# A planned attention and feed-forward block on one core: first loads keep their ranks, transfers reckoned at 0.26 MB per us, head norms off VectorE, the planner's rank shifts sought anew

## The chip, the core and the metric

The kernel runs on one core of a Trainium2 chip. The metric is the device time of one execution in microseconds (us), lower is better. Five engines work beside each other, each through its own list of instructions in a fixed order: TensorE (PE in the profile, with PEld for its weight loads), VectorE (DVE), ScalarE (ACT), GpSimd (POOL) and SyncE (SP), which here only issues DMA transfers. The engines meet through semaphores alone, so an instruction starts when its engine reaches it and every semaphore that it names has the wanted count.

## The reference

One transformer block with post-layernorm, in fp32, for 2 sequences of 512 tokens and a model width of 512.

```python
q = (x @ Wq.T)  # 32 heads of 128;  k, v: 8 heads of 128 (4 query heads share one)
q = q * rsqrt(mean(q*q) + 1e-6) * q_norm_w        # per token and head, k likewise
scores = q @ k.T / sqrt(128) + slope[head] * (key - query), keys after the query masked
out = softmax(scores) @ v @ Wo.T
x = layernorm(x + out)
h = silu(x @ gate_w.T * gate_s) * (x @ up_w.T * up_s)      # width 1376, weights are int32
x = layernorm(x + h @ down_w.T * down_s)
```

## The kernel before, in words

**Work and its pieces.** The attention part is cut by KV head `g` (0 to 7), sequence `b` (0, 1) and block `i` of 128 queries (0 to 3); a `unit` is one (g, b, i), and two neighbouring blocks make a `pair` `p`. For a pair, the projections to q, k and v are matmuls of 128 x 384; they are made by a seven-product scheme (`seven`, L747, PSUM banks `pa_q`, `pb_q`, `pc_q`), whose sums of inputs (`sx`, `tq`, and for the output projection `so`, `si`, `to`, `ti`) VectorE or GpSimd make as `tensor_tensor` operations, all at L688. The very first pair is projected plainly (`project_plain`, L867, banks `pp`). Sums such as `xT<-xT` are made in place, so a product that reads that tile waits for them.

**A head's norm.** `heads` squares a pair's projections on ScalarE (L1002), sums them per head on VectorE (L1025, tile `ms`), takes the power -0.5 on GpSimd (L674, tile `inv`), and multiplies each row by its norm: one `tensor_tensor` of 128 x 640 on VectorE or GpSimd (L1072), or five activations of 128 x 128 with a scale on ScalarE (L1065). There are 32 pairs with 2 row blocks each, so 64 such steps. The result is turned in 32 x 32 squares on VectorE (L1188) and brought into place through DRAM (`far_q` L1201, `qT` L1212).

**Scores to output.** For each unit: four score matmuls (`sc`, L1263), bias and row maximum on VectorE (L1272), exponential on ScalarE (L1288), division on ScalarE or GpSimd (L1320, L1322), squares turned on VectorE (L968, tile `st`), a trip through DRAM (`far` L977, then two loads `prT` L1385), and the product with v on TensorE (`pa`, L1408). The first units are transposed on TensorE instead (`pt`, L1359). Then the output projection (`pa_o` and its like), layernorm, and the feed-forward part (`pa_h`, `pa_d`).

**Who decides the order.** Nothing of the order is written by hand. Every operation is added to a list (`Work.add`) with a rank (`prio`; lower is earlier), the engines that may run it with a cost on each, and what it depends on. `Work.order` then plays the list through, engine by engine, with these costs: at each step it takes the operation that can start first, among equals the one of lowest rank, and so fixes both the engine and the place of each operation. DMA transfers share one lane in this play: each is reckoned at its size in MB divided by a rate, after 2.0 us of start. `Work.emit` writes the instructions in that order. Before the play, `Work.shift` is called once for each number in `SHIFTS`: the number seeds a generator that picks a stretch of ranks and adds small random amounts to the ranks in it. The numbers thus decide the order of all engines in the attention part and beyond. The lines that a sentence can't say:

```python
at, reach, by = rnd.uniform(-9, 100), rnd.choice((1, 3, 8, 30)), rnd.choice((0.1, 0.3, 1.0))
NORMED = {"DVE": dve(5 * HD) + 0.2, "POOL": pool_tt(5 * HD), "ACT": 5 * act(HD, True)}
WHO = ("DVE", "POOL", "ACT")
W.add({k: mb / 0.3 for k in queues}, prio, lambda e: fn(engine[e]), reads, writes, after)
```

**The start.** The first weights `w` (six parts on SP's queue, L486: two halves of the first quarter of depth, then the quarters), the first tokens `xT` (L512, on ScalarE's queue and later SP's), the norm weights `qw`, `kw` (L559, L560), the output weights `wo` (L541) and the tokens `acc` (L1674) have the ranks from -9.0 to -8.3. While they come, TensorE runs 14 transposes of the identity (`warm`, L554).

Of the kernel before, what the change touches and what calls it, by code (L numbers as in the profile page):

```python
# [60 lines left out]
def act(n, scaled=False):  # L61
    return 0.15 + 0.00084 * n + (0.1 if scaled else 0.0)


def dve(n):
    return 0.15 + 0.00106 * n


def pool_tt(n):
    return 0.27 + 0.00197 * n  # L70


def pool_ts(n):
# [3 lines left out]
LAG = {"PE": 0.22, "DVE": 0.1, "ACT": 0.12, "POOL": 0.2, "SP": 0.1, "ACTQ": 0.1, "NONE": 0.0}  # L77
TABLE = 1.28
SHIFTS = (
    42000001, 42000003, 42000019, 42000038, 42000046, 42000048, 42000080, 42000095, 42000168,  # L80
    42000176, 42000217, 42000257, 42000262, 42000308, 42000360, 42000448, 42000460, 42000471,
    42000478, 42000488, 42000493, 42000503, 42000508, 42000510, 42000517, 42000520, 42000530,
    42000532, 42000548, 42000582, 42000707, 42000844, 42000865, 42000884, 42000922, 42000957,
    42000970, 42000975, 42001005, 42001037, 42001049, 42001090, 42001148, 42001238, 42001283,
    42001404, 42001444, 42001471, 42001476, 42001778, 42002042, 42002048, 42002090, 42002122,
    42002149, 42002330, 42002340, 42002665, 42002784, 42002821, 42003002, 42003036, 42003133,
    42003139, 42003188, 42003348, 42003694, 42003791, 42004290, 42004466, 42005040, 42005857,
    42006497, 42006735, 42006892, 42007003, 42007117, 42007158, 42007651, 42008481, 42008514,
    42009150, 42011723, 42012356, 42012546, 42013135, 42013648, 42014108, 42014321, 42014614,
    42014976, 42015318, 42015996, 42016788, 42016932, 42017026, 42017104, 42017164, 42020579,  # L90
    42020641, 42021783, 42021971, 42022454, 42022740, 42023193, 42023363, 42024350, 42024865,
    42025415, 42026349,
)
NORMED = {"DVE": dve(5 * HD) + 0.2, "POOL": pool_tt(5 * HD), "ACT": 5 * act(HD, True)}
WHO = ("DVE", "POOL", "ACT")
ALONE = lambda p, r: False


# [65 lines left out]
class Work:  # L164
# [166 lines left out]
    def shift(self, seed):  # L331

        rnd = random.Random(seed)
        at, reach, by = rnd.uniform(-9, 100), rnd.choice((1, 3, 8, 30)), rnd.choice((0.1, 0.3, 1.0))
        moved = {}
        for o in self.ops:
            if abs(o["first"] - at) < reach:
                key = o["first"], tuple(sorted(o["costs"]))
                if key not in moved:
                    moved[key] = rnd.gauss(0, by)  # L340
                o["prio"] += moved[key]

    def emit(self):
        for seed in SHIFTS:
# [9 lines left out]
def post_ln_block(  # L354
# [22 lines left out]
    W = Work()  # L377
# [93 lines left out]
    def load(mb, prio, fn, writes, reads=(), queue="SP", after=()):  # L471
        engine = {"SP": nc.sync, "ACTQ": nc.scalar}
        queues = (queue,) if isinstance(queue, str) else queue
        W.add({k: mb / 0.3 for k in queues}, prio, lambda e: fn(engine[e]), reads, writes, after)

    w_qkv, w_o, t_q, t_o, t_i = {}, {}, {}, {}, {}

    def load_qkv(g, prio):
        w = Buf(r_w, f"w_{g}")
        w_qkv[g] = w  # L480

        def columns(kc, ns, at, queue="SP"):
            load(
                0.2 * len(ns),
                at,
                lambda q: q.dma_start(  # L486
                    w[:, kc, ns[0] : ns[-1] + 1, :], wqkv[g, :, kc, ns[0] : ns[-1] + 1, :]
                ),
                [(w, (n, kc)) for n in ns],
                queue=queue,  # L490
            )

        for kc in range(NK):
            at = prio + 0.01 * kc
            if g == 0:
                load_x(0, 0, (kc,), at, "ACTQ", 1 if kc else 2)
            if g == 0 and kc == 0:

                columns(kc, (0,), at)
                columns(kc, (1,), at + 0.001)  # L500
            else:
                columns(kc, (0, 1), at)

    def load_x(b, q, kcs, prio, queue="SP", parts=1):

        k0, k1 = kcs[0], kcs[-1] + 1
        n = NTH // parts
        for k in range(parts):
            load(
                0.13 * len(kcs) / parts,  # L510
                prio + 0.0001 * k,
                lambda e, c=k * n: e.dma_start(  # L512
                    xT[b][:, k0:k1, q * NTH + c : q * NTH + c + n], xt[b, q, :, k0:k1, c : c + n]
                ),
                [
                    (xT[b], (kc, 2 * q + m))
                    for kc in kcs
                    for m in range(k * n // P, (k + 1) * n // P)
                ],
                queue=queue,  # L520
            )
# [8 lines left out]
    def load_o(g, prio):  # L530
        if g == HKV - 1:

            flat = lambda t: t.rearrange("p j n c -> p (j n c)")[:, : 4 * DM]
            view = lambda t: flat(t).rearrange("p (m k c) -> p m k c", m=4, k=2)
            wo = Buf(r_ti, f"wo_{g}", view)
            after = [o for t in t_i.values() for o in t.users]
        else:
            after = []
            wo = Buf(r_wo, f"wo_{g}")
        w_o[g] = wo  # L540
        load(1.05, prio, lambda q: q.dma_start(wo[:, :], wot[g]), [(wo, m) for m in range(4)], after=after)  # L541
# [60 lines left out]
    order, first, past = Buf(r_prT, "order"), Buf(r_prT, "first"), Buf(r_prT, "past")  # L602
# [383 lines left out]
    def heads(p, prio):  # L986
# [67 lines left out]
        for r in range(2):  # L1054


            def normed(e, r=r):
# [16 lines left out]
            W.add(  # L1074
                {k: NORMED[k] for k in WHO},
                prio,
# [980 lines left out]
    for fc in range(NF):  # L2057
# [10 lines left out]
            after=[finished[EARLY + fc - 1]],  # L2068
# [12 lines left out]
            after=pace,  # L2081
        )
    for c in range(KF):
# [7 lines left out]
            after=[finished[EARLY + NF + c]],  # L2091
# [152 lines left out]
```

## Time and profile before

| what | value |
|---|---|
| median of 3 runs | 952.7 us (951.93, 952.7, 955.5) |
| the profiled execution, its own time | 954.71 us |
| its span, from the first to the last instruction | 952.9 us |
| mean granted TensorE clock | 0.997 |
| TensorE busy (matmul) | 940.2 us, 99% of the span, 4254 instructions |
| VectorE, ScalarE, GpSimd busy | 713.3, 485.2, 549.3 us |
| bytes moved by DMA | 157.46 MB, mean 165 GB/s |

The span is 1.8 us shorter than the time of the same execution. A row of the profile names a line, an engine and an operation, then `out<-in` by tile, shapes and a count; a number in ns is the mean of one instruction, and "idle before, <-releaser" is time in which the engine stood still just before, with what ended it. fp32 matmuls appear as two instructions each, transposes on TensorE as one. The columns of the page's slices give TensorE's granted clock in tenths, so an idle stretch and a slow clock can be told apart.

### The profile page before, as it was taken

Reading aid. Unit: us, or ns where it says so; the run is one execution under the profiler, and the core shown is the slowest. Engines: PE = TensorE matmul, PEld = TensorE weight load, DVE = VectorE, ACT = ScalarE, POOL = GpSimd, SP = SyncE. Lnnn points to the kernel's source line nnn. Section 1 sums busy time; section 2 is a strip of 40 time slices with the busy share of each in tenths; the row PEclk is TensorE's granted clock in tenths of the full one; section 3 lists DMA queues with packets and bytes.
Section 4 is the critical chain, followed back from the end, with each engine's and each line's share of the span. In section 5 each row is a group of like instructions: output and inputs, shape, how many; then the busy total and the mean of one; then the engine's idle time right before and its main releaser. Section 6 shows DMA issues by size and latency. Waiting matters only on the chain.

```text
span 952.9 us, 14098 instructions
## 1 busy us (share of the span) xinstructions
PE 940.2 (99%) x4254; PEld 682.6 (72%) x4254; DVE 713.3 (75%) x1767; ACT 485.2 (51%) x1347; POOL 549.3 (58%) x608
## 2 busy tenths in 40 slices
PE   8999999999999999999999999999999999999997
PEld 5655776766767675767677766676677888888886
DVE  7777877778877878887878888787776766675464
ACT  3676665656565656465746566565652433433100
POOL 5774775657494837775768686866564412232040
PEclk9999999999999999999999999999999999999999
DMA  9269758555583847657678786569852323310011
GB/s 324 67 199 258 232 157 241 170 184 174 176 234 107 267 132 222 206 186 198 172 239 225 235 214 190 174 184 263 217 176 81 86 81 89 85 52 23 1 45 44
DMA packets 196876, 157.46 MB, mean 165 GB/s; under 512 B 28384, under 2 KB 179680, under 8 KB 195520
## 3 DMA queue, kind: packets, MB, share of 16 engines
q1 hardware_dynamic: 195936, 155.90, 54.8%
q8 instruction: 34, 0.56, 0.2%
q10 hardware_dynamic: 864, 0.66, 0.2%
q14 instruction: 42, 0.34, 0.1%
HBM read 97.60 MB, written 58.46 MB: 164 GB/s over the span
## 4 chain that ended last, share of the span: by engine, by line
PE 96%; DMA 2%; SPq 1%; DVE 0%; issue 0%; POOLq 0%; DVEq 0%
PE pa_q L747 17%; PE sc L1263 13%; PE pa L1408 12%; PE pb_q L747 8%; PE pa_h L747 8%; PE pa_o L1632 8%; PE pb_h L747 4%; PE pc_q L747 4%; PE pb_o L1632 4%; PE pa_d L747 4%; PE pa_o L747 3%; PE pc_o L1632 2%; PE pc_h L747 2%; PE pb_d L747 2%; PE px L1440 2%; DMA prT<-far 2%
## 5 line engine op out<-in xcount | busy, mean ns | idle before, releaser
L1288 ACT ACTIVATE pr<-pr,nmax 128x48 f32<-128x48 f32 (+15 forms) x256 | 133.4, 522 | 91.2 <-DVE nmax L1272 90.1
L1263 PE MATMUL sc<-kT,qT 128*128 128x512 f32 (+15 forms) x512 | 154.1, 409 | 0.0
L1272 DVE CUSTOM_DVE_ANT_0 pr<-sc,bias 128x48 f32<-128x48 f32 (+15 forms) x256 | 109.7, 442 | 34.3 <-PE sc L1263 31.5
L1408 PE MATMUL pa<-prT,v 128*128 128x512 f32 (+1 forms) x306 | 129.6, 512 | 2.7 <-DMA prT<-far 2.7
L1263 PEld LDWEIGHTS sc<-kT,qT 128*128 128x128 f32 x512 | 88.2, 191 | 48.2 <-issue 21.9
L1320 ACT ACTIVATE pr<-pr,rden 128x64 f32<-128x64 f32 (+12 forms) x221 | 95.4, 495 | 23.1 <-DVE rden L1303 22.8
L688 DVE TENSOR_TENSOR acc<-acc,pa_o 128x512 f32<-128x512 f32 (+2 forms) x128 | 72.7, 568 | 44.9 <-PE pa_o L1632 28.2
L968 DVE STREAM_TRANSPOSE st<-pr 128x512 f32<-128x512 f32 (+1 forms) x153 | 92.1, 634 | 1.6 <-ACT pr L1320 0.6
L747 PE MATMUL pa_q<-tq,sx 128*128 128x384 f32 x248 | 90.3, 487 | 0.0
L1408 PEld LDWEIGHTS pa<-prT,v 128*128 128x128 f32 x306 | 54.0, 191 | 24.3 <-issue 6.4
L674 POOL TENSOR_TENSOR inv<-ms,nhalf 128x10 f32<-128x10 f32 (+1 forms) x33 | 64.9, 1966 | 7.8 <-DVE ms L1039 5.4
L848 ACT COPY gu<-pa_h 128x256 f32<-128x256 f32 (+1 forms) x88 | 31.8, 370 | 73.3 <-PE pa_h L747 62.7
L1002 ACT ACTIVATE sq<-c 128x640 f32<-128x640 f32 x64 | 45.7, 730 | 38.3 <-DVE c L1188 32.9
L747 PEld LDWEIGHTS pa_q<-tq,sx 128*128 128x128 f32 x248 | 45.5, 190 | 26.9 <-issue 5.5
L848 ACT COPY c<-pa_q 128x384 f32<-128x384 f32 x73 | 34.5, 473 | 54.2 <-PE pa_q L747 47.4
L1065 ACT ACTIVATE sq<-c,inv 128x128 f32<-128x128 f32 x165 | 51.9, 397 | 15.0 <-POOL inv L674 15.0
L1188 DVE STREAM_TRANSPOSE c<-sq 128x320 f32<-128x320 f32 x124 | 55.8, 485 | 0.0
L1025 DVE TENSOR_REDUCE ms<-sq 128x5 f32<-128x640 f32 x64 | 51.4, 810 | 1.2 <-ACT sq L1002 1.2
L1632 PEld LDWEIGHTS pa_o<-ti,si 128*128 128x128 f32 x336 | 43.1, 192 | 7.2 <-issue 3.6
L688 POOL TENSOR_TENSOR so<-aT,aT 128x512 f32<-128x512 f32 x23 | 29.3, 1274 | 32.8 <-PE pa_o L1632 31.7
L1322 POOL TENSOR_SCALAR pr<-pr,rden 128x64 f32<-128x64 f32 (+7 forms) x67 | 31.1, 473 | 29.4 <-DVE rden L1303 28.3
L1288 ACT ACTIVATION_READ_ACCUMULATOR pr<-pr,nmax 128x1 f32 x256 | 48.0, 188 | 0.0
(245 smaller groups left out, 2216.9 us busy)
## 6 DMA issues: line engine op xcount, KB each, us to landing
far<-st SPq DMA_DIRECT2D x122, 256.0 KB, 3.1
prT<-far SPq DMA_DIRECT2D x244, 128.0 KB, 3.2
far_q<-c SPq DMA_DIRECT2D x31, 640.0 KB, 3.9
qT<-far_q SPq DMA_DIRECT2D x62, 320.0 KB, 3.8
w<-in_wqkv_dram SPq DMA_DIRECT2D x39, 384.0 KB, 4.6
wo<-in_wot_dram SPq DMA_DIRECT2D x10, 1024.0 KB, 5.8
far<-st SPq DMA_DIRECT2D x31, 128.0 KB, 2.7
prT<-far SPq DMA_DIRECT2D x62, 64.0 KB, 3.0
```

What stands on the lines that cost most here:

```text
L674: lambda e: nc.gpsimd.tensor_tensor(dst(), src(), nhalf[:, :n], ALU.pow),
L688: lambda e: vec[e].tensor_tensor(dst(), a(), b(), alu),
L747: nc.tensor.matmul(bank[:rows, :width], lhsT=a(fa, c), rhs=b(fb, c), start=(fresh and c == 0), stop=(c == depth - 1), skip_group_check=True,)
L848: nc.scalar.copy(dst(), src())
L968: {"DVE": dve(n)}, prio, lambda e: nc.vector.transpose(dst(), src()), reads, [A(st)]
L1188: lambda e, r=r, m=m: nc.vector.transpose(cb[:, m] .rearrange("p n w -> p (n w)")[:, :half] .rearrange("p (m r h d) -> p r h m d", m=2, r= ...
L1263: lambda e, a=a, w=w, sc=sc: nc.tensor.matmul(sc[:, :w], lhsT=qT[:, r, a, : G * Q], rhs=kT[:, :w], start=True, stop=True),
L1272: lambda e, a=a, w=w, sc=sc: nc.vector.tensor_tensor_reduce(out=pr[:, a, :w], in0=sc[:, :w], in1=bias[:, S - w :], scale=-(SHRINK**-g), sc ...
L1288: lambda e, a=a, w=w: nc.scalar.activation(pr[:, a, :w], pr[:, a, :w], AF.Exp, bias=nmax[:, a : a + 1], scale=-1.0, accum_out=den[:, a : a ...
L1320: nc.scalar.activation(dst, src, AF.Copy, scale=rden[:, a : a + 1])
L1408: lambda e, j=j, prT=prT, n=n: nc.tensor.matmul(by_head(po.tile)[:, :, P - n // G :], lhsT=v[:, j, :], rhs=late(prT, j, n), start=(j == 0) ...
L1632: nc.tensor.matmul(bank[:, ts(c, P)], lhsT=a(fa, c), rhs=b(fb, c), start=fresh and c == 0, stop=True, skip_group_check=True,)
```

## The change

Four edits, of which three only feed the planner:

- the 110 numbers in `SHIFTS` are replaced by 92 others
- `Work.shift` leaves operations alone whose first rank is -8 or lower: the first loads, `warm` and their like keep the ranks that the code gives them
- `load` reckons a transfer at 0.26 MB per us instead of 0.3
- `WHO` no longer offers VectorE for a head's norm (L1072)

No operation is added or taken away. Lines from 341 on stand one line lower in the changed file; lines are named here by the file before.

```diff
 SHIFTS = (
-    42000001, 42000003, 42000019, 42000038, 42000046, 42000048, 42000080, 42000095, 42000168,
...
+    103000003, 103000004, 103000005, 103000010, 103000019, 103000029, 103000038, 103000046,
...
 )
 NORMED = {"DVE": dve(5 * HD) + 0.2, "POOL": pool_tt(5 * HD), "ACT": 5 * act(HD, True)}
-WHO = ("DVE", "POOL", "ACT")
+WHO = ("POOL", "ACT")
...
                 if key not in moved:
                     moved[key] = rnd.gauss(0, by)
-                o["prio"] += moved[key]
+
+                if o["first"] > -8:
+                    o["prio"] += moved[key]
...
-        W.add({k: mb / 0.3 for k in queues}, prio, lambda e: fn(engine[e]), reads, writes, after)
+        W.add({k: mb / 0.26 for k in queues}, prio, lambda e: fn(engine[e]), reads, writes, after)
```

## The prediction, made before the changed kernel was run

> **What bounds the kernel now.** I read the page's engine shares first, then who made TensorE wait, then the timeline where it waited.
>
> ```profile
> PE 940.2 (99%) x4254; PEld 682.6 (72%) x4254; DVE 713.3 (75%) x1767; ACT 485.2 (51%) x1347; POOL 549.3 (58%) x608
> ...
> PE pa L1408 <- DMA prT<-far: 2.7, 2, 2.1
> PE pp L867 <- DMA w<-in_wqkv_dram: 1.8, 1, 1.8
> PE warm L554 <- POOL ident masks.py:199: 1.3, 1, 1.3
> PE pb_q L747 <- DVE ms L1039: 0.5, 1, 0.5
> ```
>
> The last columns of the waits are total, times, longest. TensorE waits 6.7 us of 952.9; everything else is its own work, and no matmul is added or removed. So a new order can win little: the waits at the start (2.2 us with a 0.44 shown further below, not counting `warm`), the two on `prT`, and what the second of these costs behind it:
>
> ```profile
> 685.65 0.33 PE L1263 MATMUL sc<-kT,qT 128*128 128x64 f32 x2
> 688.09 2.05 PE L1408 MATMUL pa<-prT,v 128*128 128x512 f32 x2 [2.11 <-DMA prT<-far]
> ...
> 688.00:689.00 1.00, 0.92 (x1) 0.50 (x2) 0.00 (x0) 0.00 (x0) 0.00 (x0) 0.50 1.11 348
> ...
> 691.00:692.00 1.00, 1.00 (x4) 0.80 (x4) 0.05 (x1) 0.37 (x2) 0.00 (x0) 0.79 0.06 21
> ```
>
> In the stretches the third column from the right is the granted clock. After 2.11 us of waiting it is 0.50 for some 3.4 us, which loses 1.7 us more: 3.8 us in one place. Its cause, from the transfers of 670 to 692 us against the page:
>
> ```profile
> wo<-in_wot_dram SPq DMA_DIRECT2D x1, 1024.0 KB, 8.1
> prT<-far SPq DMA_DIRECT2D x7, 128.0 KB, 6.9
> ...
> prT<-far SPq DMA_DIRECT2D x244, 128.0 KB, 3.2
> ```
>
> A 1 MB `wo` issued at 677.6 us, right ahead of the `prT` loads, made these land in 6.9 us, not 3.2.
>
> **The start, -2.2 us.** In the built order the six `w` parts stand on SP by depth with `qw` and `kw` behind them, and ScalarE's queue has the two 128-wide `xT` parts first. Before, a 256-wide one was first and `qw`, `kw` stood ahead of a `w` part:
>
> ```profile
> 4.52 0.43 SPq L559 DMA_DIRECT2D qw<-in_qnw_dram  x1
> 5.00 0.43 SPq L560 DMA_DIRECT2D kw<-in_knw_dram  x1
> 5.47 0.43 SPq L486 DMA_DIRECT2D w<-in_wqkv_dram  x1
> ...
> 5.04 3.06 PE L867 MATMUL pp<-w,xT 128*128 128x384 f32 x8 [0.44 <-DMA xT<-in_xt_dram]
> 9.87 0.88 PE L867 MATMUL pp<-w,xT 128*128 128x384 f32 x2 [1.77 <-DMA w<-in_wqkv_dram]
> ```
>
> Changed, the first products can start when `warm` ends (1.34 + 3.25 = 4.6 us; the first transfers land at 0.72 + 3.41 = 4.1), and the last `w` part, issued near 4.6 instead of 5.47, lands near 9 us, before the 12th product asks for it at about 12 us. Both waits go: 0.44 + 1.77. Bounds -1.5 and -2.4. The loads moved back are due later: `qw`, `kw` feed only the scaling of k; the next group's `w` now stands behind the four `acc` loads, whose whole chain had landed by 27.5 us before, and is used near 43 us.
>
> **The first seven-product, +0.15 us.** `pb_q` needs `xT<-xT` from VectorE. There TensorE waited 0.51 until 20.93. It now comes 2.2 us earlier, at 18.2. VectorE's list ahead of that sum has four memsets of `pr`, four of `acc`, the bias, the `w`, `tq` sums, two `ms`: with the rows before (0.81 a sum of squares, 1.25 a `tq`, 1.82 on GpSimd between them) its end comes near 18.7, so the wait is about 0.65. GpSimd has one 1.2 us bias step ahead of the first `tq`. Bounds 0 and +1.5.
>
> **The fourth projection, +1.9 us.** New order on TensorE: `pb_q` of pair 2, six transposes, two `pa`, `pb_q` of pair 3. Between, four square turns on VectorE (1.6 us back to back from the 485 ns row, half of them after TensorE's `pb_q`), `c<-pb_q` 0.55, a `ti` sum 0.69, then GpSimd's `ti` 1.27 and `xT<-xT` 0.73, which `pb_q` needs: about 4.2 us after the first `pb_q`, against 0.7 us of transposes and 1.3 us of `pa`. So two waits, 0.5 on ScalarE's copy of `prT` and 1.7 on GpSimd. The 0.25 us that TensorE stood before a score matmul near 55 us goes. Behind the wait stand only matmuls; VectorE and ScalarE have other work. Bounds +0.5 and +2.5.
>
> **One bank used twice running, +0.8 us.** The built order has `pa_q` of pair 27 as four matmuls in a row (two products into one bank); before, none stands so. Between them: the matmul's end (0.17 behind the last issue), ScalarE's copy 0.48, two semaphores (0.04 and 0.14, as seen after such waits). Bounds 0.6 and 1.5.
>
> **`wo` moved, -3.4 us.** The second `wo` of g = 6 now stands six transfers ahead of the turns of that unit, some 14 us before the `prT` loads which it held up. The 0.61 at 648 and the 3.8 at 688 go; the same unit's `prT` stay the tightest of the new order, and I leave 1.0 there (bounds 0 and 2.4).
>
> **Norms.** 7 of 64 leave VectorE, GpSimd has 31 instead of 24, ScalarE keeps 33. The rows:
>
> ```profile
> L1072 POOL TENSOR_TENSOR sq<-c,inv x24: 1250/1256/1346, 49.4 to 666.1; 128x640 f32<-128x640 f32 x24
> L1072 DVE TENSOR_TENSOR sq<-c,inv x7: 817/820/2434, 38.9 to 523.5; 128x640 f32<-128x640 f32 x7
> ```
>
> So 0.44 us more for each of seven, 3.1 in all, on an engine busy 58%, while 26 sums go the other way to VectorE (0.42 to 0.57 us each, 75% busy). One of VectorE's seven took 2.43. The Trainium skill ("GPSIMD Engine Reference", § 4.1 Engine selection) speaks against this move: elementwise work with two inputs belongs on VectorE, GpSimd being about twice slower. The row says 1.53 times. By the rule the seven would cost 0.82 more each, 5.7 us. Either is hidden behind TensorE's next products as long as a pair is projected well ahead; without that cover 3.1 is the bound, and -1.6 the other (that one slow case). I take 0.
>
> **Rank shifts, 0.26.** They have no cost of their own beyond the order. Of waits that an order shows only on the chip I allow +1.0: the size of the 0.61 and 0.44 above.
>
> **The clock.** The Trainium skill ("TensorE: Matmul & The Clock Gate", Part 1) lets the clock drop after an idle window of about 3.4 us. The row shows it after 2.11; after 1.77 at 8.1 us none. By the rule the new 1.7 us wait costs only itself, by the row it is just below. I take 0, with +1.7 in the range.
>
> Sum: -2.2 + 0.15 + 1.9 + 0.8 - 3.4 + 0 + 1.0 = -1.75 against the profiled execution. That one took 954.7, two above the median; the runs lie in twos, near 952.3 and 955.1, and the gap is about what the `prT` wait and its slow clock cost. If the median lacks that cost, the change is worth +1 against it; if the profile adds a constant, -1.75. I take the middle, -0.7: **952.0 us**, its own range 949 to 955.
>
> **The rivals.**
> - *Two `wo` in a row* (slower). The first `wo` of g = 7 and of g = 6 now stand side by side on SP, 2 MB ahead of `far` and `prT` of unit (7, 0, 2). They wait for the last use of g = 5's weights; from there to the product that reads the new `wo` the order has seven 1.29 us products and some score matmuls, 11.1 us. One load took 5.8 (median) to 8.1, the second adds 1.05 / 0.27 = 3.9: 9.7 to 12.0. It decides once 2 MB need more than 11 us. Then some 2.5 us of waiting, 1.7 of slow clock and another 2.1 where the delayed `prT` are read: +6.3, 958.3. For it: 8.1 was seen beside turns. Against: few turns fall there.
> - *VectorE and GpSimd behind at the start*. If `pb_q` waits 2.0 and the fourth projection's wait also halves the clock: +1.35 + 1.7 + 1.7, 956.8.
> - *No surprise, and the 3.8 us is in the median too* (faster): 952.7 - 2.2 - 3.4 + 0.7 with the new waits at their lower bounds, near 947.3.
> - That the change does not do what it says is out: the built order has the loads by rank and no norm on VectorE.
>
> **How the numbers follow.** The forecast has 0.63, the two `wo` 0.17, the start 0.13, the faster case 0.07. This kernel's measurement tells 0.5% (4.8 us) from no change. The first rival falls above 957.5, of the start a quarter: slower 0.20; faster 0.07; the rest 0.73. The range takes in the start rival and most of the two `wo`: 948.5 to 958.5.
>
> **What would show it.** Right: no TensorE wait between 5 and 17 us, one of 0.3 to 1 before the first `pb_q`, about 1.7 on GpSimd's `xT` near 43 us, 0.8 on ScalarE's copy near 545, no clock of 0.50 after the start. Wrong: a wait on `wo` or `prT` near 635 to 650, a half clock behind any wait, or many small waits of scores on `kT` (norms late).

## The result, and the profile after

The changed kernel is slower by a little: median 955.21 us of 17 runs (954.07 to 957.76) against 952.70 of 17 (951.62 to 955.50), ratio 1.0029, 95% interval 1.0021 to 1.0038, which is +2.8 us (+2.0 to +3.6). The forecast was 952.0, a gain of 0.7 against the median. In the profiled executions alone there is a gain, of 0.64: 954.07 against 954.71. That difference between two profiles and two medians is half of this story.

The engines' shares on the page of the changed kernel, and its list of TensorE's waits (total, times, longest):

```profile
PE 939.7 (99%) x4254; PEld 681.8 (72%) x4254; DVE 715.4 (75%) x1772; ACT 480.9 (50%) x1334; POOL 536.0 (56%) x616
```

```profile
PE pb_q L748 <- DVE xT L689: 1.8, 1, 1.8
PE pb_q L748 <- POOL xT L689: 1.5, 1, 1.5
PE warm L555 <- POOL nhalf L548: 1.3, 1, 1.3
PE pa L1409 <- DMA prT<-far: 1.2, 1, 1.2
PE pa_q L748 <- ACT c L849: 0.6, 1, 0.6
PE pa L1409 <- ACT prT L849: 0.2, 1, 0.2
```

The waits on `w` and on the first `xT` are gone, as is one of the two on `prT`. In their places stand two on sums `xT`, one on a copy of `pa_q` and a short one on a copy of `prT`. TensorE waits 6.6 us where it waited 6.7. The timeline shows where the longer ones are:

```profile
20.46 1.53 PE L748 MATMUL pb_q<-w,xT 128*128 128x384 f32 x4 [1.79 <-DVE xT L689]
...
47.04 1.56 PE L748 MATMUL pb_q<-w,xT 128*128 128x384 f32 x4 [1.51 <-POOL xT L689]
...
552.64 1.56 PE L748 MATMUL pa_q<-tq,sx 128*128 128x384 f32 x4 [0.57 <-ACT c L849]
...
690.51 2.33 PE L1409 MATMUL pa<-prT,v 128*128 128x512 f32 x4 [1.20 <-DMA prT<-far]
```

The first line matters most. Before, the first `pb_q` began at 20.93 us, behind 2.2 us of waiting for loads and 0.51 for its sum; now it begins at 20.46. Of the 2.2 us only 0.47 have survived by then. VectorE's list in front of it says why:

```profile
11.72 2.04 DVE L689 TENSOR_TENSOR sx<-xT 128x256 f32<-128x256 f32 x1
...
18.70 0.82 DVE L1026 TENSOR_REDUCE ms<-sq 128x5 f32<-128x640 f32 x1 [0.90 <-ACT sq L1003]
19.43 0.55 DVE L689 TENSOR_TENSOR c<-pc_q,c 128x384 f32<-128x384 f32 x1
19.90 0.41 DVE L689 TENSOR_TENSOR xT<-xT 128x256 f32<-128x256 f32 x1
```

The sum `xT<-xT` needs nothing but the tokens and the first `sx`, both there by 13.8 us. It stands behind a norm's sum `ms`, which waits 0.90 for ScalarE's squares, and these wait for TensorE's last two plain products:

```profile
16.57 0.81 PE L868 MATMUL pp<-w,xT 128*128 128x384 f32 x2
```

They end at 17.38 us, before the change at 17.85: 0.47 sooner, as `pb_q` is. So the chain to the sum moved by 0.47 and not by 2.2, for two reasons. The first products ran slowly (the last section has the numbers: 1.2 us lost, against 0.3 before), and the new order puts a product into `pa_q`, 1.3 us long, ahead of these two.

### The profile page after: what moved, and what is told of

Its sections match the earlier page's. It is cut to its first block, busy times and chain, and to the rows that moved or that the text cites. A ratio compares the mean times of both kernels' runs of the same rounds, so it can differ in the third digit from the quotient of the medians.

```text
span 952.3 us, 14118 instructions
## 1 busy us (share of the span) xinstructions
PE 939.7 (99%) x4254; PEld 681.8 (72%) x4254; DVE 715.4 (75%) x1772; ACT 480.9 (50%) x1334; POOL 536.0 (56%) x616
## 4 chain that ended last, share of the span: by engine, by line
PE 97%; DVE 1%; SPq 1%; POOL 0%; DMA 0%; ACT 0%; issue 0%; POOLq 0%; DVEq 0%
PE pa_q L748 17%; PE sc L1264 13%; PE pa L1409 11%; PE pb_q L748 8%; PE pa_o L1633 8%; PE pa_h L748 8%; PE pc_q L748 4%; PE pb_h L748 4%; PE pb_o L1633 4%; PE pa_d L748 4%; PE pa_o L748 3%; PE pc_h L748 2%; PE pc_o L1633 2%; PE pb_d L748 2%; PE px L1441 2%; PE pb_o L748 1%
## 5 line engine op out<-in xcount | busy, mean ns | idle before, releaser
L1289 ACT ACTIVATE pr<-pr,nmax 128x368 f32<-128x368 f32 (+15 forms) x256 | 133.6, 523 | 77.1 <-DVE nmax L1273 75.3
L1264 PE MATMUL sc<-kT,qT 128*128 128x48 f32 (+15 forms) x512 | 152.0, 407 | 0.0
L1273 DVE CUSTOM_DVE_ANT_0 pr<-sc,bias 128x368 f32<-128x368 f32 (+15 forms) x256 | 110.5, 442 | 33.8 <-PE sc L1264 30.2
L1321 ACT ACTIVATE pr<-pr,rden 128x64 f32<-128x64 f32 (+12 forms) x208 | 90.9, 499 | 18.1 <-DVE rden L1304 17.7
L849 ACT COPY c<-pa_q 128x384 f32<-128x384 f32 x90 | 42.5, 474 | 84.1 <-PE pa_q L748 73.1
L1323 POOL TENSOR_SCALAR pr<-pr,rden 128x64 f32<-128x64 f32 (+9 forms) x80 | 36.8, 472 | 42.4 <-DVE rden L1304 35.4
L748 PE MATMUL pb_q<-w,xT 128*128 128x384 f32 x124 | 45.3, 488 | 3.3 <-DVE xT L689 1.8
L849 ACT COPY aT<-pa 128x512 f32<-128x512 f32 (+1 forms) x46 | 24.3, 529 | 46.5 <-PE pa L1409 40.0
```

What stands on the lines that cost most here:

```text
L748: nc.tensor.matmul(bank[:rows, :width], lhsT=a(fa, c), rhs=b(fb, c), start=(fresh and c == 0), stop=(c == depth - 1), skip_group_check=True,)
L849: nc.scalar.copy(dst(), src())
L1264: lambda e, a=a, w=w, sc=sc: nc.tensor.matmul(sc[:, :w], lhsT=qT[:, r, a, : G * Q], rhs=kT[:, :w], start=True, stop=True),
L1273: lambda e, a=a, w=w, sc=sc: nc.vector.tensor_tensor_reduce(out=pr[:, a, :w], in0=sc[:, :w], in1=bias[:, S - w :], scale=-(SHRINK**-g), sc ...
L1289: lambda e, a=a, w=w: nc.scalar.activation(pr[:, a, :w], pr[:, a, :w], AF.Exp, bias=nmax[:, a : a + 1], scale=-1.0, accum_out=den[:, a : a ...
L1321: nc.scalar.activation(dst, src, AF.Copy, scale=rden[:, a : a + 1])
```

## The experiments

Each kernel below takes the order that `Work.order` returns (the list `placed`) and moves a few operations in it, just before `Work.emit` writes it out; nothing is planned anew unless it is said. `move(a, behind=b)` stands for

```python
placed.remove(at[a])
placed.insert(placed.index(at[b]) + 1, at[a])     # at[n]: the n-th operation that was added
```

and the operations are named in the comment. Ratios are to the kernel before, run on the same chip; where an experiment changes the changed kernel, its gain is the difference of the two ratios, times 952.7. The changed kernel's own 1.0029 comes from other runs than these, so such a gain is good to some 1.2 us either way.

**One load elsewhere (`b_wo_behind`).** The kernel before, for the step "`wo` moved".

```diff
+move(3643, behind=3797)    # second wo of g = 6; the last prT load of unit (6, 1, 2)
```

> The kernel before, with one load moved: the second wo of g = 6 is issued behind the six prT loads of unit (6, 1, 2) instead of ahead of them. Theory P (the prediction's step): the 2.1 us wait on prT near 688 us and the half clock behind it were in the median too, so both go and the median falls by 2.5 to 3.8 us, to 949 to 950. Theory Q: the profiled execution was an unlucky one and the median hardly held this cost: the trace shows the wait gone, the median stays within 0.7 us of 952.7.

Measured: 951.82 against 952.39, ratio 0.9993 (0.9987 to 1.0), -0.7 us. The unit's own `prT` no longer keep TensorE waiting. The next unit's do; its `far` writes are issued just behind the load:

```profile
682.68 0.60 SPq L549 DMA_DIRECT2D wo<-in_wot_dram  x1
684.85 3.04 SPq L985 DMA_DIRECT2D far<-st  x3
...
694.03 1.10 PE L1416 MATMUL pa<-prT,v 128*128 128x512 f32 x2 [0.87 <-DMA prT<-far]
```

So a cost of 3.8 us that goes with the load was not in the median (theory Q, at the edge of what it allowed), and part of what was there only moved: 1.4 us of waits on `prT` are left in this trace, 0.56 near 648 and 0.87 at 694. Three other traces have the order of before at this place. In `b_first_loads` and `b_norms` the wait is 1.5 us and the clock stays at 1.00. In `b_start` it is 1.86 with a clock of 0.50 behind it, in an execution of 955.02 against a median of 952.99. The bad case is thus real, but not the usual one.

**The same load, later still (`b_wo_later`).**

```diff
+move(3643, behind=3830)    # behind the fourth prT load of unit (6, 1, 3)
```

> The kernel before, with the second wo of g = 6 issued later still: behind the first four prT loads of unit (6, 1, 3). In b_wo_behind the load only held up the turns of that next unit instead (a new wait of 0.9 at 693 us). If the load is what makes either unit late, both waits go and the time is 1.5 to 2.3 below before, near 950.5: this is then what the place costs in the median. If the turns are late without it: no more than 0.6 below before, as in b_wo_behind.

Measured: 952.27 against 952.67, ratio 0.9997 (0.9989 to 1.0005): no difference. The trace has one wait on `prT` of 1.2 us, now until 698. The expectation of 1.5 or more fell. In three positions the load leaves 2.1, 0.9 and 1.2 us of waiting on some `prT` near it, and moving it alone earns at most 1.2 us.

**The first loads alone (`b_first_loads`).** The kernel before with only this part of the change: `w` by depth ahead of `qw` and `kw`, `xT` by depth.

```diff
+# SP: six w by depth, qw, kw, then as before; ScalarE's queue: five xT by depth
```

> The kernel before, with only the first loads in the changed kernel's order: w by depth ahead of qw and kw, xT by depth with the 128-wide parts first. The prediction's step: the two waits of TensorE at 5.0 and 9.9 us go and the time falls by 2.2. Rival: the first pb_q is held by the chain of VectorE and GpSimd (in the changed kernel it began at 20.46 us, before at 20.93), so TensorE only waits later: its waits ahead of pb_q grow from 0.5 to 1.5 or 2.2 and the time falls by 0 to 0.7.

Measured: 952.46 against 952.39, ratio 1.0 (0.999 to 1.001). No gain. The waits for loads shrank to 0.2, and the wait at `pb_q` grew from 0.5 to 1.7, as the list of waits shows. The second line is from VectorE's timeline:

```profile
PE pb_q L761 <- DVE ms L1053: 1.7, 1, 1.7
...
10.98 1.50 DVE L582 SCALAR_TENSOR_TENSOR kw<-kw,qw 128x1 f32<-128x1 f32 x1 [1.08 <-DMA kw<-in_knw_dram]
```

Here there is even a second cost: `kw` lands later, and VectorE, which has its scaling ahead of the bias and of the sums, stands still for 1.08 us.

**The chain freed, in the kernel before (`b_start`).**

```diff
+# the first loads as in b_first_loads, and
+move(155, behind=70)    # sx, on GpSimd ahead of the bias steps
+move(156, behind=71)    # xT, on VectorE ahead of the tq sums
+move(157, ahead of 47)  # sx, on GpSimd
+move(49, behind=81)     # one bias step behind the first inv
```

> The kernel before with the first loads in the changed kernel's order (as b_first_loads, which gained nothing) and four sums moved up: sx, xT, sx of the first pair's partner ahead of the bias steps on GpSimd and of the tq sums on VectorE, one bias step behind the first inv. If the chain to xT was all that kept the earlier loads from paying, the wait of 1.7 at the first pb_q goes and the time falls by 1.3 to 1.8, to about 950.9. If something else is due at 18 us (the norm, the transposes of q), TensorE waits there and it stays within 0.6 of before.

Measured: 952.99 against 952.67, ratio 1.0005 (0.9996 to 1.0014). The first `pb_q` no longer waits, but the next two products do, 1.1 and 0.7, for VectorE's copy of `pa_q` and ScalarE's norm. The second answer held: in this order the sum is not the only thing on VectorE that is late.

**The chain freed, in the changed kernel (`a_xt_early`).** Its VectorE has the scaling of `kw` behind the bias and never waits for that load.

```diff
+move(156, behind=155)   # xT, right behind the first sx, on VectorE
+move(157, behind=156)   # the next sx
+move(94, behind=163)    # the first transposes of q, behind the next product
```

> The changed kernel, with the in-place sum xT and the sx behind it moved up on VectorE's list, right behind the first sx at 11.7 us (they need nothing later), and the first transposes of q put behind the next product on TensorE. If VectorE's order alone made the first pb_q wait, its 1.8 us go and the time falls by 1.5 to 1.9 against the changed kernel, to about 953.5. If the lost time comes back at a later wait of the same chain (the norm, the first scores), by under 0.5.

Measured: 954.6, ratio 1.0016 (1.0008 to 1.0023), so -1.2 against the changed kernel, less than the 1.5 to 1.9 expected but within the error of such a difference. In the trace the wait is gone whole and none stands behind it at the start:

```profile
13.82 0.42 DVE L701 TENSOR_TENSOR xT<-xT 128x256 f32<-128x256 f32 x1
...
18.81 1.45 PE L760 MATMUL pb_q<-w,xT 128*128 128x384 f32 x4
20.10 1.45 PE L760 MATMUL pa_q<-tq,sx 128*128 128x384 f32 x4
```

**The fourth projection (`a_xt3`).**

```diff
+move(405, behind=404)     # xT of pair 3, on GpSimd: ahead of a copy of vs and a sum ti
+move(406, ahead of 336)   # the sx behind it, on VectorE: ahead of two ms
```

> The changed kernel with one move: the sum xT of pair 3 two operations earlier on GpSimd, and the sx behind it ahead of two sums of squares on VectorE. The prediction put 1.7 us of waiting here; the trace shows 1.5, and 1.68 between the starts of the two matmuls. If it costs what it shows, the time falls by 1.5 to 1.7 against the changed kernel (955.2), to 953.6, ratio to before near 1.0012. If TensorE then waits later for the same chain: 954.7 or more.

Measured: 953.46, ratio 1.0009 (0.9999 to 1.0018), so -1.9 against the changed kernel: the size of the whole wait, and none comes later on that chain in the trace. This run's trace also shows what the changed kernel's profiled execution does not, a bad case at the place of `prT`:

```profile
689.86 3.63 PE L1419 MATMUL pa<-prT,v 128*128 128x512 f32 x4 [2.15 <-DMA prT<-far]
...
690.00:691.00 1.00, 1.00 (x2) 0.48 (x3) 0.76 (x5) 0.73 (x4) 0.92 (x3) 0.50 0.99 230
...
692.00:693.00 1.00, 1.00 (x2) 0.37 (x2) 0.00 (x0) 0.00 (x0) 0.00 (x0) 0.50 1.04 342
```

The granted clock (third from the right) is 0.50 for some three us behind the wait: the same event as before's at 688, in a kernel that issues its `wo` load 14 us before these `prT` loads.

**SP's queue near 680 us (`a_far`).** Between 677.3 and 681.8 us SP of the changed kernel issues six `vn` loads that nothing reads before 728. The first `st` tile of unit (6, 1, 2) is ready at 680.2 and is written only behind them, at 681.8:

```profile
677.33 4.35 SPq L1098 DMA_DIRECT2D vn<-c  x6
681.78 1.60 SPq L978 DMA_DIRECT2D far<-st  x3
```

```diff
+move(3918 to 3919, 4009 to 4012, behind=3838)   # six vn loads, behind the prT of (6, 1, 3)
+move(3800 to 3801, behind=3797)                 # the two small prT loads, behind the other four
```

> The changed kernel with SP's order alone mended near 680 us: six vn loads behind the prT loads of unit (6, 1, 3), the two small prT behind the other four. If the place costs 2 to 4 us in most executions (1.9 in the profiled one, 4.0 in the trace of a_xt3, half clock included), the time falls by 2.0 to 3.0 against the changed kernel, to 952.2 to 953.2. If it cost only what the profiled one shows: by 1.2 to 1.9.

Measured: 952.67, ratio 0.9997 (0.9989 to 1.0005), so -3.0 against the changed kernel: the place cost that in the median, though the profiled execution shows a wait of only 1.20. In this trace the first `st` is written 0.03 us after it is ready, and TensorE waits for no `prT` near 690. The run has both moves in it; of the two, `a_four` below has the small `prT` loads alone.

Two things say that the changed kernel's profiled execution was a lucky one here. The same order at this place waits 2.0 us in `a_xt_early` and 2.15 in `a_xt3`. And the mean granted clock, which every run has, fell to 0.997 or less in 6 of the changed kernel's 17 runs, in 4 of 13 of `a_xt3` and in 11 of 21 of `a_xt_early`, but in none of 13 of `a_far` and in 9 of 118 of the kernel before. A mean does not say where the clock was low; the three traces with such a mean (before, `a_xt3`, `r_who`) all have a stretch of 0.50 in mid-kernel, and so has that of `b_start`, at 0.998.

**The moves together (`a_four`, `a_six`).** `a_four` has the moves of `a_xt_early` and `a_xt3`, one `pa` ahead of the second product into `pa_q` of pair 27, and of `a_far` only the two small `prT`:

```diff
+move(2938, ahead of 3461)   # a pa of unit (5, 1, 1); the second product into the bank
```

> The changed kernel with four moves at its four places of waiting: the first xT sum early (as in the run beside it); the xT sum of pair 3 on GpSimd two operations earlier and the sx behind it ahead of the sums of squares; one pa ahead of the second product into the bank of pa_q of pair 27; the two small prT loads of unit (6, 1, 2) behind its four others. If the waits are independent, 1.8 + 1.5 + 0.6 + 1.2 us go in the profile and the time is about 950, below both kernels. If each is only the first of several on its chain, less than half of it goes: 952.5 or more.

Measured: 950.59, ratio 0.9975 (0.9964 to 0.9985), 5.1 below the changed kernel. Three of the four waits are gone from the list of TensorE's waits; at the place of `prT` they stay:

```profile
PE pa L1431 <- DMA prT<-far: 2.0, 2, 1.3
```

So the small loads alone do not mend it. `a_six` has the whole of `a_far` in it, and the transposes `pt`, whose copies made TensorE wait 0.24 near 44 us, one product earlier (`move(148, 150, ahead of 331)`).

> The changed kernel with the moves of a_four, and three more: six of the 32 KB loads vn, first read near 719 us, are issued behind the prT loads of unit (6, 1, 3), so that SP does not hold the far writes of unit (6, 1, 2) back for some 3 us; the two small prT loads as in a_four; and the two groups of transposes pt near 42 us one product earlier. If SP's queue made the two waits on prT that a_four still had (2.0 us, and a slow clock of some 0.6 behind them), they go, with 0.4 at pt: 950.6 falls to 947.6 to 948.5. If DMA bandwidth or the turns themselves set when prT lands, the waits stay within 0.7 of 2.0 and the time at 950 or more.

Measured: 948.55, ratio 0.9958 (0.9946 to 0.9971): 4.0 us below the kernel before and 6.8 below the changed one. The list of TensorE's waits has one line left:

```profile
PE warm L593 <- POOL nhalf L586: 1.3, 1, 1.3
```

**The kernel before with the moves of `b_start` and `b_wo_later` (`b_both`).**

> The kernel before with the moves of b_start and of b_wo_later together. If both kernels do the same work on TensorE and differ only in a few waits, this one ends near the changed kernel with its waits removed (a_six, 948.55): 948 to 949.5. If the order of before holds waits of its own elsewhere (0.6 near 648, 0.2 at 55), 949.5 to 950.5; over 951 if the moves disturb each other.

Measured: 953.03, ratio 1.0009 (1.0 to 1.0018), the third of the answers. Neither set of moves had paid alone, and they do not together.

**The norms alone (`b_norms`).** The seven norms of VectorE go to GpSimd in place.

```diff
+for o in placed:
+    if o["eng"] == "DVE" and "ACT" in o["costs"] and len(o["takes"]) == 3 and o["takes"][1].name.startswith("inv"):
+        o["eng"] = "POOL"
```

> The kernel before with the seven norms of VectorE given to GpSimd, at the same places of the order. The prediction's step: 0, since TensorE runs ahead of them (within 0.4 us of before). Rival: GpSimd's list holds up scores or the next norm, 0.44 us each or more: up to 3.1 us slower, with TensorE waiting for kT or GpSimd in the trace.

Measured: 952.39 against 952.44, ratio 0.9999 (0.9991 to 1.0007): nothing, with all 31 on GpSimd in the trace at the price that the row of before gave:

```profile
L1081 POOL TENSOR_TENSOR sq<-c,inv x31: 1244/1256/1490, 38.1 to 666.1; 128x640 f32<-128x640 f32 x31
```

**The same edit given to the planner (`r_who`).** `WHO` changed as in the change, the old numbers in `SHIFTS`, the play made anew.

```diff
-WHO = ("DVE", "POOL", "ACT")
+WHO = ("POOL", "ACT")
```

> The kernel before, its own numbers in SHIFTS, with WHO alone changed: the play is made anew and the whole order with it. If the numbers are tied to the settings they were found under, the order has many new waits: slower by 3 to 10 us, with waits in places that neither kernel has. If they are a good order for either setting: within 1.5 us of before.

Measured, in 4 runs: 970.86 against 952.44, ratio 1.0185 (1.0167 to 1.0203), 17.6 us slower, far above the 3 to 10 expected. TensorE waits in places that neither kernel has, the three largest totals being:

```profile
PE pa L1408 <- DMA prT<-far: 3.4, 3, 1.6
PE pa_q L747 <- ACT c L848: 2.4, 5, 0.6
PE pb_o L747 <- POOL aT L688: 1.9, 1, 1.9
```

The edit itself costs nothing (`b_norms`); the order that the play makes of it costs 18 us. So a part of such a change, planned alone, tells nothing of that part.

## Why the prediction was wrong, step by step

- **Start, -2.2: this step failed.** "Both waits go" was right, and the last `w` landed at 9.5 us, near the 9 forecast. That the gain stays was wrong. TensorE was ready for `pb_q` 1.75 us sooner than before, but its wait there grew by 1.28, since the sum `xT` stands on VectorE behind squares of the last plain products. Alone the loads earn 0.0 (within 1.0). "`qw`, `kw` feed only the scaling of k" overlooked that this scaling stands on VectorE ahead of the sums; with the earlier loads in before's order it waited 1.08.
- **The first seven-product, +0.15: the other half of the same error.** I summed VectorE's durations to 18.7; it was 20.3. A sum of busy times does not hold the two waits for ScalarE's squares (0.85 and 0.90): the last squares were there only at 18.67, and three operations, 1.6 us in all, lie between them and the end of `xT`. TensorE's wait was 1.79 against 0.65.
- **The fourth projection, +1.9: right.** The waits are 1.51 and 0.24, less the 0.25 at 55 us that went: 1.5, within the bounds. The move of its `xT` part alone was worth 1.9 (`a_xt3`, within 1.2), and the engine was named, GpSimd.
- **One bank twice, +0.8: right.** The wait is 0.57 and the matmul starts 0.73 late. In `a_four` it is gone, among other moves; alone it was not tried.
- **`wo` moved, -3.4: this step failed, and most of the miss lies here.** Two things were wrong. The 3.8 us of the profiled execution are not the usual cost: with the load out of the way the kernel before gains 0.7. And 1.0 was left for the place in the changed order; it costs 3.0 (`a_far`), now through SP's `vn` loads ahead of the `far` writes (moving the small `prT` loads alone did not mend it), which the prediction did not look at. What the place cost before was not measured whole. An estimate is the 0.7 and the 1.4 of waits on `prT` that were left in `b_wo_behind`, some 2.1; the step is then worth about +0.9, not -3.4.
- **Norms, 0: right** (`b_norms`). The rule against GpSimd (the Trainium skill, "GPSIMD Engine Reference", § 4.1 Engine selection) did not decide, nor did its factor of 2 against the rows' 1.53: the norms lie beside other work.
- **Unseen waits, +1.0: none came.** The changed kernel's list shows none but these.
- **The step from one execution to the median failed too.** The forecast named both readings, +1 "if the median lacks that cost" and -1.75 if it does not, and took "the middle, -0.7" (the middle of the two is -0.4). The first was nearer to what came. Before's profiled execution lies 2.0 above its median, the changed kernel's 1.1 below: the lowest of its 17.

Put together for the medians: 0.0 (start and first seven-product) + 1.9 (fourth projection) + 0.7 (one bank, by its wait) + 0.9 (`wo` and `prT`, the estimate above) + 0 (norms) = 3.5; measured 2.8. With parts that are good to some 1.2 each this agrees, and no more than that can be read from it.

Of the rivals, "VectorE and GpSimd behind at the start" had the right place and nearly the right wait (2.0 forecast, 1.79 found), without the half clock that it added; "two `wo` in a row" did not happen: there is no wait near 640. The third adds up to 947.8, not 947.3.

## What to carry to other kernels

Here a load that came sooner earned only what the next chain on the way left over. Follow that chain on its own engine, waits included, and look for an operation in it that stands behind one it does not need. One profiled execution can hold a stall of 4 us that most executions do not have, and another can miss a usual one. Where a forecast rests on a single wait, read it as a range, and ask what else on the same queue can make that unit late. In a planned order, take the order as it came out and move the few operations at its waits by hand: five places mended were worth 6.8 us, where one edit planned anew cost 18.

## What the runs showed of the hardware

**The first products run at half pace while the clock column says 1.00.** With no pause behind `warm`, the first products of the changed kernel start 0.64 us apart up to 6.3 us and 0.32 from 6.9 on, a loss of 1.2 that the prediction did not have; before lost about 0.3. A stretch of this time, with the granted clock third from the right, and the row of these products (min, median, max in ns):

```profile
4.40:5.00 0.60, 0.60 (x2) 0.32 (x2) 0.33 (x2) 0.00 (x0) 0.00 (x0) 1.00 0.90 256
...
L868 PE MATMUL pp<-w,xT x32: 486/486/847, 4.4 to 16.9; 128*128 128x384 f32 x32
```

What slows them is not shown.

**Whether the clock halves behind a wait is not settled by the wait's length.** It did after 2.11 us (before), 2.15 (`a_xt3`), 1.86 (`b_start`) and 1.22 (`r_who`, half a us after the wait), and did not after 1.97 (`a_xt_early`) and 1.79 (changed kernel). In `r_who` the wait and a stretch behind it, and then a stretch of `a_xt_early` behind its wait:

```profile
636.42 1.95 PE L1263 MATMUL sc<-kT,qT 128*128 128x304 f32 x4 [1.22 <-POOL kT L1228]
...
638.00:639.00 1.00, 1.00 (x3) 0.53 (x2) 0.59 (x3) 0.56 (x3) 0.00 (x0) 0.50 0.04 8
```

```profile
690.00:691.00 1.00, 0.79 (x2) 0.30 (x2) 1.00 (x8) 0.82 (x3) 0.92 (x2) 1.00 1.07 330
```

So a wait of one to two us cost itself, or itself and 1.7 more: added up over stretches of 1 us, the slow time is 3.4 us in each of the four. The Trainium skill ("TensorE: Matmul & The Clock Gate", Part 1) has the clock rise after a busy and fall after an idle window of about 3.4 us, and lets these windows run free of the kernel. The length of the four slow stretches fits such a window, and that the windows run free would fit the changing length of the slow start. That the window has to be idle throughout does not fit drops after 1.22 to 2.15 us, and here the measurement decides. No run here moved a wait against the windows.

**A short VectorE operation can last until the GpSimd sum beside it ends.** `sx<-xT` took 2.04 us, from 11.72 to 13.76, beside GpSimd's `tq` from 11.66 to 13.47; the next such sum took 0.42. Before, a bias step did the same (2.01, from 9.93, beside `tq` from 9.86 to 11.66). In `a_xt_early` the `sx` starts at 13.37, when `tq` ends (13.44), and takes 0.41; there it is one step of the scaling of `kw`, begun at 11.68, that lasts until 13.45. The Trainium skill ("Trainium Architecture — The Big Picture", "What this means for kernel authors") says that the two share a port pair as an exclusive lock, which these times fit; no run here took the `tq` away.
